# One scattered row per token instead of two, and every instruction placed anew, in a sparse attention layer on one core

## The chip, the cores and the metric

The kernel runs on one core of a Trainium2 chip. The metric is the time of one execution on the device in microseconds (us). The same program is executed several times; the median of the runs is given, and one execution is also recorded by the hardware profiler. Engines are named as in the profile: PE (TensorE), PEld (its weight loads), DVE (VectorE), ACT (ScalarE), POOL (GpSimd), SP (SyncE, which here only issues DMAs).

## The reference

There are 16 batches of 1024 tokens with 512 numbers each, and one 1024 x 1024 adjacency for all of them, in which every token has itself and a few neighbours.

```python
h = jnp.maximum(_layernorm(x, axis=-1), 0.0)
q = (h @ Wq + bq).reshape(b, n, 8, 64)      # k and v in the same way
scores = jnp.einsum('bihd,bjhd->bhij', q, k) / jnp.sqrt(64.0)
mask = jnp.where(adj == 0, -1e9, 0.0)
weights = softmax(scores + mask, axis=-1)
out = x + jnp.einsum('bhij,bjhd->bihd', weights, v)
```

Everything is in float32. Most of a row of the adjacency is zero, so that the softmax of a token runs over a handful of neighbours.

## The kernel before

**Sorting, once.** Tokens are sorted by their number of neighbours and cut into 8 tiles of 128. A tile t has `CAPS[t]` slots for neighbours, (11, 8, 6, 5, 4, 3, 3, 2), so that tiles of small degree do little. To sort, the kernel reads the adjacency, takes the degree of each token on DVE, and finds the rank of each token (`rank_of`, `ranks`), which is its row in sorted order. For each natural tile t of 128 tokens, `list_of(t)` (L1120, L1121) masks the rows of the adjacency with token numbers and takes the eight largest with one MAX8: the list of up to eight neighbours. Two facts about each token then have to go to its place in sorted order, through DRAM:

- the numbers: the token's own number and, for the first batch only, the two constants of its layernorm, scale and shift (`shift` computes the last). `tell(t)` scatters them, three floats for a token, into `told_table`;
- the list: whether the token is its own neighbour, and the eight neighbours. `spread(t)` scatters them, nine floats for a token, into `lists_table`.

Both are indirect DMAs that POOL issues (L1124), one for each tile and table, so sixteen. Once all eight of a table are done, `collect` (L1135) loads the table back in sorted order with one DMA of SP's queue. From the numbers, `perm_of` (L1142) makes `perm`, the list of token numbers in sorted order. With `perm`, POOL loads the tokens of all batches in sorted order (`load_x`, L1002), one indirect DMA for each tile, writes the results back (`put_out`, L1409), and fetches the adjacency rows of the longest tile again (`long_rows`, L1152), whose remaining neighbours are found by `long_blocks` and `longest`. From the lists, `spots` (L1147) and `slots` (L1240 and following) make `index`, the row numbers that the gathers use. While all this goes on, the first batch's k and v are computed in natural order (names that end in `_first`) and scattered by rank (L1095).

**Each batch.** For each of 8 tiles: layernorm (DVE sums, ACT L1037), four transposes by PE (`flip`, L1044), a copy of the transposed tile by ACT (`unflip`, L1049), and projections to k, v and q (`project`: a bias product L1055 and four float32 products L1057, which the profile counts as eight). The k and v of a tile go into one of three DRAM buffers of 1024 rows. Then the attention runs in 14 `UNITS` for a batch, a unit being up to four slots of one tile: `gather` (L1288) fetches the k|v rows of the neighbours, one indirect DMA for each slot, the own row by SP; DVE multiplies with q (L1298) and sums to scores (L1302); ACT takes exponents (L1306) and weighs v, eight activations for a slot (`weigh_s`, L1332), some slots by DVE (`weigh_v`, L1318); DVE, POOL and PE add the slots up (`fold` L1337, `add_up` L1356); DVE divides, and POOL or DVE adds x (`residual`, L1406). Tile 0 has a unit more, for tokens with more neighbours than slots (`pieces`, number -1). The projections of a batch run one batch ahead of its attention.

**The order of work.** It is written out by hand. Each operation has a place, a number in the table `PLACES`; `Plan.ordered()` sorts all operations by it and issues them in that order, and an engine executes its own in the order of issue. The kind `once` holds the sorting, `first` the natural-order k and v, `0`, `1` and `2` the first three batches, `3` every further one but two, `next` the last but one, `last` the final one; for batch b the number gets b times `PERIOD` = 95.290021 added. Waits between engines come from the dependencies.

Of the kernel before, what the change touches and what calls it, by code (L numbers as in the profile page):

```python
# [97 lines left out]
        list_of=(-13.2, -13.4, 13.93, 14.05, -4.33, -7.76, -9.88, 14.25,),  # L98
        tell=(-12.63, -16.97, -13.14, 9.24, 0.89, 16.11, 17.75, 19.88,),
        spread=(45.38, 47.45, 30.7, 45.48, 45.35, 30.46, 22.54, 45.26,),  # L100
        collect=(-9.17, 5.02,),
        others=(14.42,),
        perm_of=(0.42,),
        spots=(26.84,),
        long_rows=(30.4,),
        long_blocks=(16.58, 20.59, 22.61, 24.22, 24.98,),
        longest=(27.18, 29.37, 32.28, 35.43, 36.11, 39.52, 41.52, 44.79, 45.14,),
        count_pieces=(46.89,),
        first_piece=(122.72,),
        owners=(94.07,),  # L110
        flip_owners=(136.43,),
        copy_owners=(113.68,),
        list_pieces=(137.27,),
        pieces=(127.38,),
        slots=(142.24,),
        add_bias=(-19.2, -17.6,),
        spread_bias=(68.07,),
        copy_bias=(89.7,),
# [4 lines left out]
        norm=(75.49, 76.09, 77.09, 77.49, 79.89, 80.09, 80.34, 80.69,),  # L123
        flip=(75.49, 75.69, 76.49, 76.69, 78.69, 78.89, 90.39, 104.64,),
        unflip=(75.89, 76.49, 77.29, 77.89, 80.49, 80.72, 96.22, 97.88,),
        proj_kv=(75.89, 77.49, 76.29, 77.89, 76.89, 78.49, 79.09, 79.29, 86.87, 98.15, 99.79, 107.75, 135.06, 147.6, 153,
            148.32,),
        evict_kv=(76.89, 79.29, 77.69, 79.49, 78.09, 80.29, 80.4, 80.66, 96.1, 96.13, 96.42, 106.28, 154.55, 162.49, 169.71,
            172.46,),
        store_kv=(78.35, 116.17, 119.38, 125.35, 140.7, 146.55, 148.18, 147.06,),  # L130
        variance=(75.89, 76.89, 79.29, 81.69,),
        power=(75.69, 76.29, 78.29, 87.8,),
# [3 lines left out]
        load_x=(30.09, 30.5, 38.8, 45.21, 45.44, 47.92, 49.07, 49.69,),  # L136
        norm=(2.13, 2.31, 24.77, 49.09, 71.39, 77.14, 77.27, 78.66,),
        flip=(50.32, 51.95, 54.11, 55.9, 60.64, 67.45, 67.52, 68.48,),
        unflip=(27.69, 53.06, 72.64, 77.2, 79.54, 81.13, 82.77, 84.23,),
        queries=(67.49, 69.07, 115.56, 126.07, 127.49, 138.29, 148.67, 168.76, 169.97,),  # L140
        gather=(45.09, 65.92, 63.96, 81.66, 82.98, 67.8, 87.05, 86.63, 69.01, 87.14, 102.98, 103.26, 67.61, 108.86, 109.63,
            108.64, 107.92, 79.49, 116.69, 119.1, 130.36, 131.45, 130.44, 102.76, 142.21, 138.67, 142.4, 144.98, 150.63,
            142.37, 142.46, 108, 152.91, 152.09, 152.7, 153.37, 153.1, 152.82, 153.23, 171.08, 171.84, 155.19, 172.79,
            155.41, 171.17, 171.11,),
        multiply=(47.46, 64.59, 81.01, 107.03, 126.74, 113.33, 126.77, 141.63, 149.43, 155.18, 163.45, 170.22, 180.88,
            178.07,),
        score=(47.54, 67.41, 96.06, 111.76, 129.2, 117.87, 128.06, 146.83, 153.31, 155.84, 165.66, 174.39, 181.78, 195.93,),
        exponent=(92.19, 93.82, 105.44, 111.15, 115.51, 115.42, 115.56, 141.97, 143.4, 152.67, 166.31, 172.53, 173.27,
            183.23,),
        row_sums=(64.37, 70.18, 97.04, 118.27, 142.77, 160.52, 163.48, 203.64,),  # L150
        share=(64.49, 74.75, 101.56, 119.16,),
        weigh_v=(69.44, 130.54, 142.01, 144.6, 161.03, 163.57, 170.25, 175.36, 195.82,),
        weigh_s=(92.85, 101.83, 100.44, 95.75, 106.78, 112.94, 106.75, 115.48, 115.39, 115.45, 122.29, 116.89, 121.19, 119.7,
            142.94, 135.53, 142.97, 143.03, 144.58, 154.99, 152.31, 153.27, 163.13, 166.52, 165.91, 171.8, 172.93, 171.74,
            173.08, 173.04, 172.99, 174.92, 175.62, 181.86, 185.22, 185.42, 187.44,),
        fold=(71.91, 97.01, 97.07, 132.47, 137.68, 138.95, 141.69, 143.23, 145.64, 143.05, 153.79, 155.15, 156.82, 161,
            163.76, 171.2, 173.85, 175.66, 181.17, 186.5, 187.92, 183.84, 200, 202.21, 204.35, 204.53,),
        residual=(109.25, 124.53, 138.45, 141.77, 153.19, 171.14, 178.55, 219.35,),
        put_out=(129.95, 130.51, 141.35, 142.43, 153.4, 178.16, 179.5, 225.23,),
        join=(147.89, 161.06, 175.01,),  # L160
        scale=(148.16, 161.67, 176.53, 211.41,),
        copy_q=(145.23,),
        add_up=(188.54, 194.88, 203.87, 205.55,),
        more=(201.41,),
        pass_on=(203.77,),
        seen=(331.72,),
    ),
    1: dict(
        load_x=(-45.57, -43.85, -39.73, -39.1, -35.32, -8.38, 7.1, 14.11,),
        stats=(-63.36, -61.71, -54.75, -49.26, -50.34, -20.16, 1.69, 45.35,),  # L170
        norm=(-12.29, -8.07, -1.29, 11.92, 17.92, 21.28, 45.19, 45.66,),
        flip=(-14.6, 13.76, 33.62, 50.55, 65.56, 72.21, 73.87, 79.53,),
        unflip=(-6.21, -2.22, 15.4, 21.31, 28.65, 37.54, 57.61, 68.73,),
        proj_kv=(17.02, 20.04, 31.75, 42.81, 49.67, 52.6, 71.12, 55.79, 72.24, 74.1, 74.46, 79.5, 79.61, 83.24, 86.3, 90.4,),
        evict_kv=(-2.01, -35.87, 14.8, 20.07, 20.47, 37.41, 38.89, 36.39, 47.71, 60.13, 57.69, 63.79, 70.59, 76.3, 77.5,
            77.55,),
        store_kv=(7.84, 6.03, 7.72, 17.75, 21.65, 22.37, 41.88, 46.5,),
        variance=(-59.83, -48.24, 0.42, 46.54,),
        power=(-31.44, 7.33, 34.59, 50.93,),
        shift=(-56.77, -25.47, 22.23, 52.69,),  # L180
        queries=(92.98, 95.46, 99.76, 113.88, 114.01, 119.61, 134.23, 135.77, 151.42,),
        gather=(53.63, 85.6, 64.02, 85.49, 85.7, 72.03, 102.18, 95.44, 87.81, 104.49, 108.17, 108.68, 107.7, 109.8, 109.4,
            111.58, 112.73, 107.63, 119.79, 126.28, 135.9, 135.96, 135.93, 140.28, 147.73, 148, 149.33, 149.5, 150.8, 150.83,
            149.71, 142.94, 156.83, 157.14, 151.75, 157.7, 150.86, 150.89, 162.73, 165.24, 165.07, 165.98, 165.43, 166.72,
            176.54, 166.09,),
        multiply=(100.67, 106.6, 119.91, 124.46, 149.54, 145.64, 149.6, 154.01, 164.31, 168.95, 171.4, 175.59, 182.84,
            188.66,),
        score=(107.36, 108.32, 124.43, 142.56, 149.57, 145.7, 153.22, 157.27, 165.13, 170.5, 171.68, 182.66, 188.41, 193.53,),
        exponent=(101.25, 100.12, 106.42, 110.23, 116.2, 116.09, 136.58, 137.26, 142.79, 164.86, 172.22, 183.82, 187.9,
            189.8,),  # L190
        row_sums=(111.52, 118.48, 124.49, 145.67, 151.53, 163.54, 171.43, 223.45,),
        share=(112.04, 119.71, 124.55, 145.84,),
        weigh_v=(115.89, 145.87, 155.15, 158.81, 169.44, 171.46, 193.56, 188.61, 193.59,),
        weigh_s=(102.16, 107.3, 103.87, 104.01, 107.98, 108.93, 112.16, 116.05, 121.06, 115.46, 125.94, 135.88, 136.78,
            122.78, 137.3, 139.07, 140.95, 141.59, 137.36, 163.59, 164.34, 153.33, 167.75, 166.89, 171.97, 181.76, 182.84,
            176.37, 187.96, 186.35, 188.1, 189.16, 190.92, 190.49, 191.49, 191.11, 190.86,),
        fold=(119.37, 124.52, 136.3, 135.99, 136.05, 152.83, 147.47, 157.39, 160.24, 157.34, 165.19, 168.14, 169.06, 169.41,
            174.3, 178.51, 174.7, 177.42, 193.62, 193.65, 193.68, 198.47, 195.72, 204.29, 208.27, 212.87,),
        residual=(113.65, 130, 143.43, 153.45, 160.4, 179.56, 185.95, 209.42,),
        put_out=(129.97, 136.02, 156.67, 157.96, 166.22, 183.18, 187.67, 215.86,),  # L200
        join=(163.89, 169.49, 187.98,),
        scale=(164.12, 171.36, 188.49, 227.3,),
        copy_q=(144.08,),
        add_up=(188.22, 192.32, 197.88, 215.67,),
        more=(188.38,),
        pass_on=(191.08,),
        seen=(236.64,),
    ),
    2: dict(
        load_x=(-56.28, -51.47, -39.61, -36, -12.07, 6.83, 6.86, 40.79,),  # L210
# [34 lines left out]
        copy_q=(156.1,),  # L245
        add_up=(202.93, 206.57, 210.96, 218.78,),
        more=(187.77,),
        pass_on=(211.16,),
        seen=(311.13,),
    ),  # L250
    3: dict(
# [1356 lines left out]
```

## Time and profile before

| what | value |
|---|---|
| median of 3 runs | 1613.55 us (1610.17 to 1617.66) |
| profiled execution, own time | 1612.02 us |
| its span | 1609.9 us |
| mean granted PE clock | 0.992 |
| PE busy | 1572.1 us |
| DVE busy | 1518.2 us |
| ACT busy | 1444.8 us |
| POOL busy | 1258.7 us |

The span is the time between the first and the last instruction in the trace; the profiled execution's own time has some 2 us more around it. The busy time of an engine is a sum over the whole span. Register, branch and DMA-issuing instructions do not count as busy, except the indirect DMAs of POOL, which appear with the time that POOL spends on issuing them. The granted clock says how much of its full speed PE was allowed. Times within a timeline are counted from the start of the span.

### The profile page before, as it was taken

The page shows a single profiled execution, that of the slowest core. Times are in us where ns is not written, and L with a number is a line of the kernel's source. Part 1 is how long each engine was busy: PE and PEld are TensorE (multiplying, and loading weights), DVE is VectorE, ACT ScalarE, POOL GpSimd, SP SyncE. Part 2 cuts the span into 40 slices and gives each one's busy share as a digit, 9 for nine tenths or more (in the row PEclk, how much of TensorE's full clock was granted, in tenths as well). Part 3 has the DMA queues.
Part 4 walks back from the last instruction along what each step waited for, and adds up shares of the span by engine and source line. Part 5 has one row for each costly group of instructions (what it writes and reads, how often), then busy time and mean ns, then how long its engine had stood idle before and what let it go on. Part 6 is the DMA issues. An engine that isn't in the chain of part 4 may idle for free. (4 is left out here: it accounts for less than half of the span.)

```text
span 1609.9 us, 19515 instructions
## 1 busy us (share of the span) xinstructions
PE 1572.1 (98%) x4242; PEld 732.0 (45%) x4242; DVE 1518.2 (94%) x2075; ACT 1444.8 (90%) x5428; POOL 1258.7 (78%) x1185
## 2 busy tenths in 40 slices
PE   8999999999999999999999999999999999999687
PEld 4444444444444444444444444444444444444233
DVE  8889999999999999999999999999999999999897
ACT  4459999898999989899898989999998998989897
POOL 3777778887788888888788787878788887786666
PEclk9999999999999999999999999999999999999899
DMA  6499989999999999999999999999999999998886
GB/s 249 141 351 341 334 319 358 329 366 323 341 333 345 366 333 357 325 351 349 339 357 346 345 337 345 344 343 352 330 339 331 341 373 326 338 335 330 324 306 217
DMA packets 149876, 531.56 MB, mean 330 GB/s; under 512 B 19052, under 2 KB 19052, under 8 KB 149752
## 3 DMA queue, kind: packets, MB, share of 16 engines
q0 software_dynamic: 109840, 390.70, 67.9%
q1 hardware_dynamic: 39912, 139.56, 23.0%
q8 instruction: 35, 0.57, 0.1%
q14 instruction: 89, 0.73, 0.1%
HBM read 429.46 MB, written 100.72 MB: 329 GB/s over the span
## 5 line engine op out<-in xcount | busy, mean ns | idle before, releaser
L1332 ACT ACTIVATE g<-g,weights 128x64 f32<-128x64 f32 x4704 | 1160.3, 338 | 40.9 <-DVE weights L1311 37.8
L1288 POOL DMA_INDIRECT g<-kv,index x608 | 642.2, 1056 | 206.7 <-issue 163.2
L1057 PE MATMUL pq<-wq,hT 128*128 128x512 f32 x1024 | 462.4, 595 | 0.0
L1057 PE MATMUL pk<-wk,hT 128*128 128x512 f32 x960 | 431.7, 593 | 0.0
L1057 PE MATMUL pv<-wv,hT 128*128 128x512 f32 x960 | 431.4, 593 | 0.0
L1302 DVE TENSOR_REDUCE weights<-g 128x32 f32<-128x2048 f32 (+2 forms) x224 | 423.7, 1897 | 2.0
L1298 DVE TENSOR_TENSOR g<-g,pq 128x2048 f32<-128x2048 f32 (+2 forms) x208 | 388.7, 1870 | 28.1 <-DMA g<-kv 9.9
L1057 PEld LDWEIGHTS pq<-wq,hT 128*128 128x128 f32 x1024 | 195.8, 191 | 216.9 <-issue 213.2
L1057 PEld LDWEIGHTS pv<-wv,hT 128*128 128x128 f32 x960 | 182.4, 190 | 213.5 <-issue 210.6
L1057 PEld LDWEIGHTS pk<-wk,hT 128*128 128x128 f32 x960 | 182.7, 190 | 201.4 <-issue 196.8
L1337 DVE TENSOR_TENSOR g<-g 128x512 f32<-128x512 f32 (+1 forms) x301 | 253.9, 851 | 9.8 <-ACT g L1332 8.4
L1409 POOL DMA_INDIRECT out_dram<-x,perm x128 | 136.7, 1068 | 39.8 <-issue 30.6
L1002 POOL DMA_INDIRECT x<-in_x_dram,perm x128 | 135.8, 1061 | 34.9 <-issue 32.5
L1337 POOL TENSOR_TENSOR g<-g 128x512 f32<-128x512 f32 x90 | 115.0, 1284 | 17.6 <-DVE g L1337 10.5
L1037 ACT ACTIVATE h<-x,shift,rstd 128x512 f32<-128x512 f32 x120 | 96.5, 807 | 12.0 <-DVE shift L1027 11.4
L1318 DVE TENSOR_TENSOR g<-g,weights 128x512 f32<-128x512 f32 x143 | 101.9, 716 | 1.1 <-ACT weights L1306 0.6
L1356 PE MATMUL acc<-g,ident 128*128 128x512 f32 x170 | 84.4, 612 | 14.6 <-ACT g L1332 10.8
L1044 PEld LDWEIGHTS pht<-ident,h 128*128 128x128 f32 x512 | 63.2, 141 | 68.6 <-issue 52.7
L1406 POOL TENSOR_TENSOR x<-x,o 128x512 f32<-128x512 f32 x64 | 81.9, 1280 | 9.4 <-DVE o L1392 5.0
L1049 ACT COPY hT<-pht 128x512 f32<-128x512 f32 x128 | 73.0, 571 | 16.3 <-PE pht L1044 16.2
L1011 DVE BATCH_NORM_STATS2 st<-x 128x6 f32<-128x512 f32 x120 | 81.2, 677 | 1.6 <-DMA x<-in_x_dram,perm 1.6
L1044 PE MATMUL pht<-ident,h 128*128 128x128 f32 x512 | 76.5, 273 | 3.2 <-ACT hT L1049 1.9
(242 smaller groups left out, 1080.2 us busy)
## 6 DMA issues: line engine op xcount, KB each, us to landing
g<-kv SPq DMA_DIRECT2D x128, 512.0 KB, 7.7
kv<-kvt SPq DMA_DIRECT2D x120, 512.0 KB, 6.9
g<-kv,index POOLq DMA_INDIRECT x608, 6.9
adj<-in_adj_dram SPq DMA_DIRECT2D x8, 512.0 KB, 8.2
x_first<-in_x_dram SPq DMA_DIRECT2D x8, 256.0 KB, 6.0
x<-in_x_dram,perm POOLq DMA_INDIRECT x128, 5.5
out_dram<-x,perm POOLq DMA_INDIRECT x128, 6.6
wk<-in_L_gnn_Wk_dram SPq DMA_DIRECT2D x1, 1024.0 KB
```

Source lines behind the costliest of these rows:

```text
L1002: nc.gpsimd.indirect_dma_start(out=X[n][:], out_offset=None, in_=x_rows, in_offset=on(ap=perm[:, t : t + 1], axis=0), element_offset=b * N * D
L1037: nc.scalar.activation(HN[n], X[n], AF.Relu, bias=shift, scale=scale)
L1044: nc.tensor.transpose(PH[n][:, c, :], hn[:, ts(c, P)], ident)
L1057: nc.tensor.matmul(pt, HT[n][:, c, :], W[name][:, c, :], start=(apart and c == 0), stop=(n != -NT and c == DC - 1))
L1288: nc.gpsimd.indirect_dma_start(out=G[i][:, s].rearrange("p j d -> p (j d)"), out_offset=None, in_=KV[b % len(KV)][:], in_offset=on(ap=inde ...
L1298: nc.vector.tensor_tensor(k, k, Q[b, t][:, None, :].to_broadcast([P, count, D]), ALU.mult)
L1302: nc.vector.tensor_reduce(weights[:, w, :], heads(G[i][:, :count, 0, :]), AX.X, ALU.add)
L1318: nc.vector.tensor_tensor(v, v, own.to_broadcast([P, n, H, HD]), ALU.mult)
L1332: nc.scalar.activation(v[:, h, :], v[:, h, :], AF.Identity, scale=weights[:, c + s, h : h + 1])
L1337: engine.tensor_tensor(v[:, 0:n], v[:, 0:n], v[:, first : first + n], ALU.add)
L1356: nc.tensor.matmul(ACC[b, home], owner_t if t < 0 else ident, v[:, s, :], start=(u == added_up(b, B, home)[0] and s == 0), stop=(u == adde ...
L1409: nc.gpsimd.indirect_dma_start(out=out_rows[t], out_offset=on(ap=perm[:, t : t + 1], axis=0), in_=X.pop(b * NT + TILES.index(t))[:], in_of ...
```

## The change

The two tables become one of twelve floats for a token: own number, scale, shift, whether it is its own neighbour, eight neighbours. `spread` is gone; `tell(t)` scatters the twelve floats at once, eight indirect DMAs instead of sixteen, and so depends on `list_of(t)` and on `shift`. One `collect` loads the table back, and both `perm_of` and `spots` depend on it. The list columns stand behind the numbers, in columns 3 to 11. Besides, every number in `PLACES` is replaced, of all kinds from `once` to `last`. `PERIOD`, the buffers, the units and the division of work among engines stay as they are, and a steady batch issues the same instructions as before.

```diff
     for t in range(NT):
         add(("list_of", t), "DVE", [("ends",), ("no_diagonal", t)], [sources])
-        add(("tell", t), "POOL", [("ranks",), ("shift", (t - NT) // 2)])
-        add(("spread", t), "POOL", [("list_of", t)])
-    add(("collect", "told"), "SP", [("tell", t) for t in range(NT)])
-    add(("collect", "lists"), "SP", [("spread", t) for t in range(NT)])
+        add(("tell", t), "POOL", [("list_of", t), ("shift", (t - NT) // 2)])
+    add(("collect",), "SP", [("tell", t) for t in range(NT)])
...
-    add(("perm_of",), "DVE", [("collect", "told")])
-    add(("spots",), "DVE", [("collect", "lists"), ("setup", 2)])
+    add(("perm_of",), "DVE", [("collect",)])
+    add(("spots",), "DVE", [("collect",), ("setup", 2)])
...
-        itself, near = 0, slice(1, 9)
-        width_of = dict(told=3, lists=9)
...
+        itself, near = 3, slice(4, 12)
+        before, after = (const.tile([P, NT, 12], F32, tag=name, name=name) for name in ("before", "after"))
+        table = nc.dram_tensor("told_table", [N, 12], F32).ap()
+        views = dram_disjoint_views(table, NT)
...
-                nc.gpsimd.memset(before["lists"], 0.0)
-                nc.gpsimd.tensor_copy(before["told"][:, :, own], place)
+                nc.gpsimd.memset(before, 0.0)
+                nc.gpsimd.tensor_copy(before[:, :, own], place)
...
+        def tell(t):
             nc.gpsimd.indirect_dma_start(
-                out=views[name][t], out_offset=on(ap=spot_i[:, t : t + 1], axis=0), in_=before[name][:, t, :], in_offset=None
+                out=views[t], out_offset=on(ap=spot_i[:, t : t + 1], axis=0), in_=before[:, t, :], in_offset=None
             )
...
-        def collect(name):
-            nc.sync.dma_start(after[name], tables[name].rearrange("(p t) c -> p t c", t=NT))
+        def collect():
+            nc.sync.dma_start(after, table.rearrange("(p t) c -> p t c", t=NT))
```

And of the places, the sorting's one of the steady batches' (kind `3`) and two of the last batch's:

```diff
-        list_of=(-13.2, -13.4, 13.93, 14.05, -4.33, -7.76, -9.88, 14.25,),
-        tell=(-12.63, -16.97, -13.14, 9.24, 0.89, 16.11, 17.75, 19.88,),
-        spread=(45.38, 47.45, 30.7, 45.48, 45.35, 30.46, 22.54, 45.26,),
-        collect=(-9.17, 5.02,),
-        others=(14.42,),
-        perm_of=(0.42,),
-        spots=(26.84,),
-        long_rows=(30.4,),
+        list_of=(-13.2, -13.4, -13.64, -5.49, 29.82, -11.73, -13.5, 9.88,),
+        tell=(-2.47, -2.81, -2.2, 0.46, 20.99, -0.47, 0.43, 15.84,),
+        collect=(-3.23,),
+        others=(32.93,),
+        perm_of=(31.19,),
+        spots=(32.96,),
+        long_rows=(26.22,),
...
-        flip=(-10.81, -8.95, 19.94, 35.21, 52.47, 61.74, 70.98, 73.85,),
+        flip=(-7.65, -5.54, 33.09, 40.88, 46.68, 59.19, 70.43, 81.4,),
...
-        queries=(262.15, 252.79, 252.44, 222.65, 210.97, 194.72, 156.92, 125.39, 127.47,),
+        queries=(296.72, 265.33, 253.44, 241.69, 218.97, 184.96, 182.93, 120.67, 143.27,),
...
-        copy_q=(115.48,),
+        copy_q=(139.29,),
```

Of the last three pairs, `flip` is of the kind `3`, one number for each tile from 7 to 0; `queries` and `copy_q` are of the kind `last`.

## The prediction

> **What bounds the kernel now.** I read the page's busy times first, then the same by stage, then the timeline of each engine at the two ends. In the page, the busy line and the slices:
>
> ```profile
> PE 1572.1 (98%) x4242; PEld 732.0 (45%) x4242; DVE 1518.2 (94%) x2075; ACT 1444.8 (90%) x5428; POOL 1258.7 (78%) x1185
> ...
> PE   8999999999999999999999999999999999999687
> ```
>
> TensorE is the full engine, and only the first slice and the last three fall below nine tenths. By stage (columns: window, length, busy PE, PEld, DVE, ACT, POOL, granted clock, DMA share, GB/s; instruction counts in brackets):
>
> ```profile
> 0.00:113.00 113.00, 104.90 (x311) 51.48 (x312) 94.55 (x263) 51.41 (x105) 70.10 (x90) 0.98 0.68 245
> 685.00:780.00 95.00, 95.00 (x258) 44.41 (x257) 90.59 (x119) 89.37 (x340) 78.13 (x73) 1.00 0.95 351
> 1447.00:1543.00 96.00, 77.82 (x191) 34.01 (x190) 87.19 (x85) 85.50 (x332) 62.59 (x60) 0.91 0.87 323
> 1543.00:1610.00 67.00, 56.88 (x139) 24.94 (x137) 54.35 (x73) 54.20 (x230) 44.42 (x43) 0.97 0.73 257
> ```
>
> In the middle PE has no gap: one batch costs the PE work of one batch, about 95.3 us (24 projections of 8 x 0.429 + 0.215 = 3.65, 8 flips of 0.44, the rest adds and small products). Time can be won or lost in three ways: PE starts its steady run later or earlier; it comes to wait inside that run; or the last 107 us, where PE idles 96 - 77.8 + 67 - 56.9 = 28 us and DVE and ACT are at 81 to 91%, get shorter or longer.
>
> **What the Trainium skill says.** "DMA: Bandwidth & Descriptors", section on the SWDGE path, fits a DMA's time as about 2.0 us plus bytes/436e3. A scatter of 128 rows of 12 B lands after 2.4 us at the median in this trace, one of 36 B after 2.4 too, so a 48 B row should cost no more. "TensorE: Matmul & The Clock Gate", section on the clock gate, has PE at half rate after an idle window of about 3.4 us and at full rate after about as long busy. The trace agrees in kind: after a gap of 9.2 us two adds took 2.05 us, 0.86 elsewhere. But a gap of 1.91 us too was followed by a projection of 5.19 us instead of 3.60.
>
> **Part 1: eight scatters fewer.** On POOL (start, us, instruction, idle before):
>
> ```profile
> 45.91 0.96 POOL L1124 DMA_INDIRECT told_table<-before_told,spot_i  x1 [0.30 <-issue]
> ...
> 70.86 0.96 POOL L1124 DMA_INDIRECT lists_table<-before_lists,spot_i  x1 [0.30 <-issue]
> ...
> 87.15 1.01 POOL L1288 DMA_INDIRECT g<-kv,index  x1 [0.19 <-issue]
> ```
>
> Each takes 0.96 + 0.30 = 1.26 us of POOL; eight are 10.1 us. All lie before the first gather, in a stretch where POOL issues back to back. On SP two collects become one (a load of 2.7 us either way; 384 B for each partition instead of 96 and 288). The zeroing of 128 x 96 values instead of 128 x 72 is early work on POOL ahead of the ranks, under the wait for the adjacency: nothing.
>
> **Part 2: the permutation waits for the lists.** Before, `perm_of` needed the numbers only. DVE shows both collects:
>
> ```profile
> 50.73 0.17 DVE L1142 CAST perm<-after_told 128x8 int32<-128x8 f32 x1 [2.30 <-DMA after_told<-told_table]
> ...
> 76.12 0.75 DVE L1147 COPY spot<-after_lists 128x8 f32<-128x8 f32 x7 [1.73 <-DMA after_lists<-lists_table]
> ```
>
> Now one row carries both, and the last tile's list must be found first. The lists cost 1.21 + 1.23 = 2.4 us of DVE each; the first ends near 38.8, and in the new order of DVE all eight run with little between them, so the last (tile 4) ends near 55.7. Its scatter is issued at 55.8, lands 2.1 later, the collect takes 2.7: `perm` at about 60.6, **10 us later** than 50.73. DVE waits about 4.9 us for it (before: 2.30 and 1.73). Behind it on DVE stand only `others`, spots and slots, then the layernorm sums of loads that need `perm` themselves; behind the collect on SP stand the own rows of the first gathers, not due before 80. Behind `perm` on POOL stand the store of three k|v tiles that were not waiting for it, then `long_rows` and the eight loads of batch 0. Nine issues of 1.27 us give 62.2 to 72.3 for them (before: the first eight loads at 53.2 to 74.7, with scatters between). So the first loads are later and the last ones earlier. Spots and slots now follow `perm` at once (62 to 66 instead of 76 to 80).
>
> PE in this stretch: the sixteen projections of batch 0's k and v in natural order run to about 76 in both orders. Then before had
>
> ```profile
> 79.08 0.66 PE L1044 MATMUL pht<-ident,h 128*128 128x128 f32 x4 [1.91 <-ACT hT L1049]
> ...
> 79.89 5.19 PE L1057 MATMUL pq<-wq,hT 128*128 128x512 f32 x8
> ...
> 102.53 0.39 PE L1055 MATMUL pq<-bias_parts,chosen 128*128 128x512 bf16 x1 [0.70 <-DVE g L1298]
> ```
>
> that is 1.91 + 1.6 (clock) + 0.70 = 4.2 us lost. In the new order I follow the flips of batch 0: a load lands 5.5 us after its issue, the norm takes 0.81 and the flip waits on it, and I find gaps of about 2.5, 1.4 and 0.6 us, 4.5 us, plus up to 2 of lost clock. **The start of the steady run moves by 0 to +3 us; I take +2.** A loss of 10 us (the whole delay of `perm`) is excluded as long as PE has the natural-order projections to do until 76.
>
> **Part 3: the first gather.** POOL has ten fewer microseconds of issues but two natural k|v stores wait for ACT's evictions; I get the first gather at 82.5 instead of 87.15 and the first multiply at 91.4 instead of 96.45. PE does not wait for the attention there; only the 0.70 us behind the multiply can come from it. By the fourth multiply (113.5 in both) the lead is gone, since the new order of DVE puts more layernorm work between. Worth nothing by itself.
>
> **Part 4: places of the steady batches.** Each batch issues the same instructions; only their order on each engine changes. What decides is whether PE meets an operand that is not ready. Counting PE work between the end of a flip and the projection that reads it, the shortest distance of a steady batch is 4.94 us now (tile 1) and in the new order 4.09 (tile 7, now 7.74), beside 4.94 again. In between ACT must copy the flipped tile (0.57 us, L1049) and, being in order, finish what it has begun; one neighbour slot is eight activations, 2.02 us in this trace. With one slot ahead 4.09 - 0.57 - 2.02 leaves 1.5 us; with two it is 0.5 short. One early batch of the kernel before has a distance of 4.09 too, and PE waits nowhere there. The other distances are 7.3 us and more, and projections of queries reach PE at nearly the same points as before (that of the pieces 3.7 us later). I take **0**, from 0 to +25 (a stall of up to 2 us in 13 batches); a gain is excluded, since PE has no gap to lose there.
>
> **Part 5: the tail.** The last k|v projection ends at 1503.7. Now
>
> ```profile
> 1512.91 2.05 PE L1356 MATMUL acc<-g,ident 128*128 128x512 f32 x2 [9.20 <-ACT g L1332]
> ...
> 1515.76 4.06 PE L1057 MATMUL pq<-wq,hT 128*128 128x512 f32 x8
> ```
>
> so the last batch's first query sits on PE behind an add that waits 9.2 us for ACT, and the multiply behind it waits once more for ACT's copy of that query:
>
> ```profile
> 1524.93 2.29 DVE L1298 TENSOR_TENSOR g<-g,pq 128x2048 f32<-128x2048 f32 x1 [4.98 <-ACT q L1279]
> ```
>
> In the new order the query stands directly behind the last projection, and the multiply waits for its gathers alone, which land near 1521 if they are issued as now (first at 1508.75). That is 4 us earlier on DVE. After 1543 DVE and ACT share the limit, so some is given back: **-3 us**, bounded by -6 (DVE's whole 4.98 and a warm PE clock) and +4 (DVE and ACT left with a worse interleaving of 14 units).
>
> **Sum.** 1612.0 (profiled execution: span 1609.9 and 2.1 around it) + 2 + 0 - 3 = 1611. The median shown is 1613.55, 1.5 above that execution, so the middle of my case is 1611 to 1612.5; I say 1612.
>
> **Rivals.** *Slower:* ACT stands two or three slots behind at the flip of tile 7 (or an equal distance elsewhere that a schedule with 90% busy ACT and 95% busy DVE cannot hold). From the point at which the wait passes 0.6 us a batch, 13 batches make more than 8 us; at 1 us it is 1612 + 13 = 1625, at 1.5 us 1632. For it: DVE and ACT leave only 5 us of slack in a batch and every position is new. Against it: in the trace of before PE waits nowhere between 110 and 1503 at the same kind of distances. *Faster:* the earlier gather is kept to the first batch's end (5 us), and the tail gives the full 4: 1613.5 - 9 = 1604. Against it: PE's clock, not DVE's, sets the steady run, so a lead at the start has no way to the end. *Late permutation:* the loads that come 10 us later leave PE without flips at 76: +5 and a cold clock, 1618, still inside the band of no change.
>
> **Numbers.** What a measurement of this kernel can tell from no change is about 0.5%, 8 us. No change (cases of the sum and of the late permutation): 0.46, own range 1606 to 1620. Slower, by stalls of PE or a longer tail: 0.36. Faster: 0.18. The range goes from 1603 to 1630.
>
> **What would show it.** Right: `perm` near 60 us; sixteen scatters become eight; first gather near 82; PE without gaps from about 115 to 1504; the first multiply of the last batch near 1521. Wrong: PE waits on ACT's flipped tile or on an eviction in the windows of the middle, a window of 95 us that holds less than 95 us of PE, or a tail longer than 107 us after the last k|v projection.

## The result and the profile after

The changed kernel takes 1620.17 us (median of 8 runs, 1618.75 to 1623.73), the kernel before, run beside it, 1616.29 us (8 runs). The ratio is 1.0036, with a 95% interval of 1.0020 to 1.0053: **slower by 0.36%**, about 6 us. A second set of the changed kernel gave 1621.37 us and again 1.0036 [1.0024, 1.0048]. The forecast was 1612 us, a hair faster than before; the measured time lies inside its range, on the other side. The profiled execution took 1619.76 us, with a span of 1618.1, near its median; that of before (1612.02) lies 1 to 4 us under the medians of its kernel. So the two traces differ by 8.2 us of span where the medians differ by 4 to 6. In one later set (e16 and e17 below) the kernel before took 1631.1 us, 15 to 18 us more than in all others, for a reason that no trace here shows, and e17, the changed kernel with one operation moved, was 0.4% faster than it: the 0.36% holds for the other sets.

The busy line of the page, and stages of the changed kernel (columns as in the prediction: window, length, then busy PE, PEld, DVE, ACT, POOL, granted clock, DMA share, GB/s):

```profile
PE 1573.4 (97%) x4209; PEld 731.5 (45%) x4242; DVE 1516.5 (94%) x2075; ACT 1447.7 (89%) x5428; POOL 1247.9 (77%) x1177
```

```profile
0.00:113.00 113.00, 103.05 (x304) 50.41 (x309) 91.28 (x255) 52.44 (x106) 62.18 (x81) 1.00 0.66 242
208.00:303.00 95.00, 93.90 (x251) 43.53 (x254) 89.55 (x111) 87.53 (x331) 73.80 (x70) 1.00 0.92 338
303.00:398.00 95.00, 91.80 (x248) 42.40 (x248) 90.23 (x112) 87.22 (x329) 74.31 (x69) 1.00 0.89 325
683.00:778.00 95.00, 94.89 (x256) 44.34 (x257) 91.40 (x119) 89.47 (x342) 76.90 (x72) 1.00 0.94 342
```

The middle is as full as before. POOL has eight instructions less and 11 us less work. What is new is the stretch from 208 to 398 us: PE is idle for 95 - 93.90 + 95 - 91.80 = 4.3 us there. The same windows of the kernel before:

```profile
208.00:303.00 95.00, 94.80 (x257) 44.07 (x256) 90.29 (x119) 89.80 (x346) 77.58 (x71) 1.00 0.94 340
303.00:398.00 95.00, 94.88 (x258) 44.10 (x257) 92.68 (x117) 86.91 (x330) 76.18 (x72) 1.00 0.94 341
```

0.3 us. In the second trace of the changed kernel (c_after below) it is 3.7 us. The timeline of PE shows the two longest of these waits, in batches 2 and 3:

```profile
319.56 0.39 PE L1048 MATMUL pq<-bias_parts,chosen 128*128 128x512 bf16 x1 [1.67 <-DVE g L1285]
343.02 3.70 PE L1050 MATMUL pv<-wv,hT 128*128 128x512 f32 x8 [1.17 <-ACT kvt L1068]
```

A query waits for a DVE multiply that still reads the PSUM bank of an earlier query, and a projection to v waits for ACT's copy out of the k|v bank that it is to take. Neither waits for a flipped tile.

To see where the time sits, one PE instruction of each batch serves as a mark, the query of the pieces (tile -1). Before and then after, for batches 0 and 3:

```profile
155.67 1.02 PE L1275 MATMUL pq_-1_1404<-q,owner 128*128 128x512 f32 x2
...
440.63 1.02 PE L1275 MATMUL pq_-1_3801<-q,owner 128*128 128x512 f32 x2
```

```profile
160.14 1.02 PE L1262 MATMUL pq_-1_1423<-q,owner 128*128 128x512 f32 x2
...
449.62 1.02 PE L1262 MATMUL pq_-1_3843<-q,owner 128*128 128x512 f32 x2
```

The new order has one projection more ahead of the mark (3.65 us), so of the 4.47 us by which it is later at batch 0 0.82 were lost at the start. In the same way the loss is 1.65 us at batch 1, 4.8 at batch 2 (two projections more there), 5.34 at batch 3 and 5.77 at batch 8; the last k|v projection ends at 1508.77 us instead of 1503.71. After it the changed kernel needs 109.3 us to the end of the span, the kernel before 106.2. **The account of the pair of traces: start +0.82, batches 1 to 3 (from the mark of batch 0 to that of batch 3) +4.52, the rest of the run about -0.3, the end +3.1, together 8.2.** It is one pair of executions; which of these sums come again in other traces is said below.

At the end, on PE and DVE of the changed kernel:

```profile
1508.82 3.60 PE L1050 MATMUL pq<-wq,hT 128*128 128x512 f32 x8
```

```profile
1524.15 2.28 DVE L1285 TENSOR_TENSOR g<-g,pq 128x2048 f32<-128x2048 f32 x1
...
1543.51 2.29 DVE L1285 TENSOR_TENSOR g<-g,pq 128x2048 f32<-128x2048 f32 x1 [3.22 <-issue]
...
1551.62 2.27 DVE L1285 TENSOR_TENSOR g<-g,pq 128x2048 f32<-128x2048 f32 x1
```

The query is where the prediction saw it, directly behind the last projection. The first multiply starts 15.4 us after that projection's end (before: 21.2), the fourth, which waits 3.22 us, after 34.7 (35.6), the fifth after 42.8 (41.9). The fifth of the kernel before:

```profile
1545.58 2.28 DVE L1298 TENSOR_TENSOR g<-g,pq 128x2048 f32<-128x2048 f32 x1
```

The lead of 5.8 us is gone within four units, and the rest is behind.

### The profile page after: what moved, and what is told of

The parts are those of the page before. It is cut to its first block, busy times and chain, and to the rows that moved or that the text cites. A ratio compares the mean times of both kernels' runs of the same rounds, so it can differ in the third digit from the quotient of the medians.

```text
span 1618.1 us, 19496 instructions
## 1 busy us (share of the span) xinstructions
PE 1573.4 (97%) x4209; PEld 731.5 (45%) x4242; DVE 1516.5 (94%) x2075; ACT 1447.7 (89%) x5428; POOL 1247.9 (77%) x1177
## 5 line engine op out<-in xcount | busy, mean ns | idle before, releaser
L1319 ACT ACTIVATE g<-g,weights 128x64 f32<-128x64 f32 x4704 | 1164.9, 347 | 34.7 <-DVE weights L1298 31.3
L1275 POOL DMA_INDIRECT g<-kv,index x608 | 634.3, 1043 | 215.9 <-issue 162.0
L1285 DVE TENSOR_TENSOR g<-g,pq 128x1536 f32<-128x1536 f32 (+2 forms) x208 | 389.1, 1871 | 20.8 <-DMA g<-kv 5.8
L1396 POOL DMA_INDIRECT out_dram<-x,perm x128 | 141.5, 1106 | 39.9 <-issue 30.0
```

Of the source, the lines that this page charges most:

```text
L1275: nc.gpsimd.indirect_dma_start(out=G[i][:, s].rearrange("p j d -> p (j d)"), out_offset=None, in_=KV[b % len(KV)][:], in_offset=on(ap=inde ...
L1285: nc.vector.tensor_tensor(k, k, Q[b, t][:, None, :].to_broadcast([P, count, D]), ALU.mult)
L1319: nc.scalar.activation(v[:, h, :], v[:, h, :], AF.Identity, scale=weights[:, c + s, h : h + 1])
L1396: nc.gpsimd.indirect_dma_start(out=out_rows[t], out_offset=on(ap=perm[:, t : t + 1], axis=0), in_=X.pop(b * NT + TILES.index(t))[:], in_of ...
```

## The experiments

Two theories stood at first. The places theory: one table costs nothing, and the new numbers in `PLACES` lose the time, in batches 1 to 3 and at the end. The table theory: the permutation, 11 us later, makes the first batches late, and PE pays for that. (Not quite every number in `PLACES` is new: some 120 of about 1950 are the same in both kernels, nearly all of them of the sorting and of the first loads ahead of the lists.)

"Before" is the median of the kernel before on the same chip at the same time.

| kernel | us | before | ratio, 95% interval |
|---|---|---|---|
| e1_table_only | 1625.95 | 1614.95 | 1.0074 [1.0060, 1.0088] |
| e2_places_only | 1654.20 | 1614.95 | 1.0242 [1.0220, 1.0263] |
| e3_after_old_end | 1687.83 | 1614.95 | 1.0470 [1.0452, 1.0488] |
| e4_after_old_ramp | 1724.06 | 1614.95 | 1.0677 [1.0662, 1.0691] |
| e5_after_ramp_moves | 1620.43 | 1613.82 | 1.0039 [1.0027, 1.0051] |
| e6_before_last_query | 1614.08 | 1613.82 | 0.9992 [0.9984, 1.0001] |
| e7_after_unit_order | 1619.76 | 1613.82 | 1.0035 [1.0022, 1.0047] |
| e8_table_stores_first | 1624.04 | 1613.82 | 1.0052 [1.0036, 1.0068] |
| e9_table_hidden | 1622.35 | 1615.22 | 1.0043 [1.0027, 1.0058] |
| e10_before_first_multiply | **1609.21** | 1615.22 | **0.9965 [0.9953, 0.9977]** |
| c_after | 1621.37 | 1615.22 | 1.0036 [1.0024, 1.0048] |
| e11_after_evictions_early | 1620.06 | 1613.17 | 1.0041 [1.0026, 1.0057] |
| e12_after_outputs_early | 1619.65 | 1613.17 | 1.0044 [1.0029, 1.0060] |
| e13_after_both | 1621.25 | 1613.17 | 1.0047 [1.0035, 1.0060] |
| e14_less_act | 1621.52 | 1614.13 | 1.0045 [1.0024, 1.0066] |
| e15_less_dve | 1615.76 | 1614.13 | 1.0013 [1.0001, 1.0024] |
| e16_dve_time_back | 1623.52 | 1631.10 | 0.9952 [0.9937, 0.9968] |
| e17_others_early | 1623.88 | 1631.10 | 0.9960 [0.9942, 0.9978] |

e16 and e17 are read by their traces alone.

**The table without the new places (e1, e8, e9).** e1 has the table of the changed kernel and the places of before, with what the dependency demands:

```diff
-        tell=(-12.63, -16.97, -13.14, 9.24, 0.89, 16.11, 17.75, 19.88,),
-        spread=(45.38, 47.45, 30.7, 45.48, 45.35, 30.46, 22.54, 45.26,),
-        collect=(-9.17, 5.02,),
+        tell=(-12.63, -13.0, 14.0, 14.1, 0.89, 16.11, 17.75, 19.88),
+        collect=(5.02,),
...
-        perm_of=(0.42,),
+        perm_of=(14.3,),
```

> One table of twelve floats, one scatter for each tile, all places as before, except that perm_of stands behind the last list and the scatters behind their lists. Places theory (the new numbers in PLACES cost the time, the table costs nothing): within 2 us of before; perm at 58 to 62 us instead of 50.7, yet PE without waits from 115 us on, and the last k|v projection ends at 1502 to 1506 us. Table theory (perm eleven us later makes the layernorms of the first batches late, and PE waits for what depends on them): 4 to 8 us slower than before, with PE waits of 3 us or more between 208 and 398 us.

It lost 11 to 12 us, so the places theory failed here. But the time was not lost where the table theory had it: from 208 to 398 us PE was idle for 0.1 us. Nearly all of it lies ahead of 115 us, at one wait on PE's timeline:

```profile
65.18 0.58 PE L1048 MATMUL pk_first<-bias_parts,chosen 128*128 128x512 bf16 x1 [12.41 <-ACT kvt_first L1068]
```

ACT's copy of a natural-order k waited for a buffer, whose scatter stood on POOL behind scatters of the table, which waited for the last list. e8 moves three such stores ahead:

```diff
+MOVED = {('store_kv', -7): 0.5, ('store_kv', -6): 0.6, ('store_kv', -5): 0.7}
-            result.append(PLACES[kind][spot[0]][at] + PERIOD * (b or 0))
+            result.append(MOVED[key] if key in MOVED else PLACES[kind][spot[0]][at] + PERIOD * (b or 0))
```

> As e1_table_only, with the scatters of three natural k|v tiles ahead of the table's scatters on POOL, in time in which POOL waited for a list. If e1 lost its time because those stores, standing behind scatters that wait for the last list, kept ACT's eviction and so PE waiting (12.4 us): that wait falls below 2 us and the whole is 8 to 12 us faster than e1, about as before or a little slower. If it lost it to the late permutation itself: PE then waits for the flips of batch 0 instead, and it is less than 4 us faster than e1.

The 12.4 us wait is gone, the time is not: against before, e8 is 1 to 4 us better than e1, and PE now waits for the flips of batch 0, 5.05 and 2.85 us, whose tokens are loaded by the permutation at 63.8 us. This is the second answer of its expectation. e9 besides puts the natural-order work of PE and ACT ahead of these flips, as the changed kernel does:

```diff
+    ('proj_kv', -2, 1): 17.0, ('proj_kv', -1, 1): 27.5, ('flip', 0): 41.4, ('proj_kv', -1, 0): 42.1, ('flip', 1): 42.3,
+    ('evict_kv', -2, 0): 2.0, ('evict_kv', -2, 1): 2.05, ('norm', 0): 4.1, ('norm', 1): 14.6, ('unflip', 0): 15.5,
...
```

> As e8_table_stores_first, and besides, PE and ACT do what they have left of the natural k and v ahead of the first flips and norms of batch 0, as in the changed kernel: seven operations of PE and fifteen of ACT change places, all before 95 us; every later place is that of before. Places theory (the table is free where other work covers the wait for the permutation, and the changed kernel loses its 6 us later, in batches 1 to 3 and at the end): within 3 us of before, at 1612 to 1617 us, PE idle below 1.5 us between 113 and 398 us, 106 us after the last k|v projection. Table theory: still 5 us or more slower than before.

Still 0.43% slower, and all of it ahead of 113 us (0.3 us idle from 208 to 398 us, 105.4 us after the last k|v projection). PE's largest wait is further back now, at another flip of batch 0:

```profile
97.32 2.30 PE L1060 MATMUL pht<-ident,h 128*128 128x128 f32 x8 [6.08 <-ACT h L1053]
```

So one table costs 7 to 12 us in an order made for two, in the three ways tried. The changed kernel's own order of the start pays 0.82 for it. A new order of the start is thus part of the price of the table; that every later place had to change too is not shown.

**The places without the table, and places of two kernels joined (e2, e3, e4).** e2 takes the places of all batches from the changed kernel and the rest from before, e3 and e4 put kinds of before into the changed kernel. As orders of different kinds don't fit, `ordered()` was changed in them so that, where no engine's next operation can be issued, the ready operation with the least place leaves its queue early.

```diff
+            if not ready:
+                for engine, queue in waiting.items():
+                    for i in queue[head[engine] :]:
...
+                _, i, new = min(ready)
```

> Two tables and sixteen scatters, and the sorting's own places, as before; the places of every batch, the first to the last, as in the changed kernel. Places theory: 4 to 8 us slower than before, PE waits of 3 us or more between 208 and 398 us on evictions and on a multiply, the last k|v projection ends at 1507 to 1510 us, the rest after it takes 109 us. Table theory: within 2 us of before.

> The changed kernel with the places of the last two batches as before. Places theory, in which 3 of the us are lost after the last k|v projection: 3 us faster than the changed kernel (1617 us at 1620 for that), the last k|v projection still at 1507 to 1510 us, the rest after it 106 us instead of 109.3. Rival (the end is set by what all engines still have to do, whatever the order, and the 3 us are the spread of single executions): as the changed kernel, the rest 109 us.

> The changed kernel with the places of the first three batches (kinds 0, 1, 2) as before. Places theory: PE's waits between 208 and 398 us (4.3 us in the changed kernel) fall below 1 us, the last k|v projection ends at 1503 to 1506 us instead of 1508.8, and the whole is 3 to 5 us faster than the changed kernel. Table theory: the waits stay, no faster.

All three missed every expectation by far, at the seams: e2's PE is idle for 13.4 us between 113 and 208 us, e3's for 20.3 between 1348 and 1443, e4's for 20.0 between 113 and 208 and for 25.5 between 303 and 398. Their times say nothing on the theories; they say that the places of one kind hold only beside the neighbours that they were made for.

**The waits of batches 1 to 3 (e5, e11).** In the changed kernel, six of 33 k|v projections between 205 and 400 us find their bank freed only 0.05 to 0.33 us before they take it; in the kernel before none does, and the least margin is 0.87 us. (Margin: from the end of the eviction, which is the copy out of the bank, to the first float32 product of the next projection into that bank, the second one further on; counted from the two traces.) e5 moves three evictions and one query (its list is shown), e11 sixteen evictions on ACT by one to seven steps, one on DVE, and the same query:

```diff
+MOVED = {('queries', 2, 1): 342.0, ('evict_kv', 27, 0): 339.15, ('evict_kv', 17, 1): 221.65, ('evict_kv', 22, 1): 273.0}
```

> The changed kernel with four operations moved by one to four steps in their own engine's order, so that none of the four largest waits of PE between 208 and 398 us (0.47, 0.42, 1.67 and 1.17 us) has its cause left: three evictions ahead of the weighting or the multiply they stood behind, one query behind one k|v projection. Places theory: those waits go, the last k|v projection ends 3.0 to 3.7 us earlier, at about 1505.3 us, and the whole is about 3 us faster than the changed kernel. Rival (DVE and ACT are late there altogether, the waits only come up a few steps later): other waits of PE take their place, and the whole stays within 1 us of the changed kernel.

> The changed kernel with sixteen evictions of batches 1 to 3 moved ahead of the weighting that they stood behind on ACT (by one to seven steps), one on DVE, and one query behind one k|v projection on PE. Bank theory (PE takes one of two k|v banks back 0.1 to 0.4 us after its eviction in six places, and a late eviction stops it): PE's waits between 113 and 398 us fall from 3.8 to 4.4 us to below 1.5, the last k|v projection ends 2.5 to 3.5 us earlier, and the whole is 2.5 to 3.5 us faster than the changed kernel. Rival (DVE and ACT are late altogether): other waits take their place, no faster.

Both came out as their rivals say. PE's idle time between 208 and 398 us stayed at 4.2 and 4.5 us, with other waits; in e11 two of them are for k|v banks that ACT has not left:

```profile
342.21 3.70 PE L1072 MATMUL pv<-wv,hT 128*128 128x512 f32 x8 [1.72 <-ACT kvt L1090]
...
346.99 0.38 PE L1070 MATMUL pk<-bias_parts,chosen 128*128 128x512 bf16 x1 [1.07 <-ACT kvt L1090]
```

**Which engine is late there (e14, e15).** Each takes work from one engine in batches 0 to 2 and leaves every order as it is.

```diff
-            for h in range(H):                                            # e14, weigh_s
+            for h in range(0 if b < 3 and s == 0 and count == 4 else H):
+            if b < 3:                                                     # e15, weigh_v
+                return
+            if n == 2 and i < 3 * NU:                                     # e15, fold
+                return
```

> The changed kernel; in batches 0 to 2 the first slot of each unit of four slots is left unweighed: ACT has 6 slots of 2.0 us less to do in each of these batches, DVE all of its own. If ACT is the late engine in the early batches: PE's waits between 113 and 398 us fall from 3.8 to 4.4 us to below 1.5 and the last k|v projection ends about 3 us earlier. If DVE is: the waits stay above 3 us.

> The changed kernel; in batches 0 to 2 DVE leaves out its own weighting of v and the first fold of each unit of four slots, some 13 us of DVE in each of these batches; ACT does all of its own. If DVE is the late engine: PE's waits between 113 and 398 us fall below 1.5 us. If ACT is: they stay above 3 us. If both e14 and e15 take them away, each engine waits for the other, and the order couples them.

The two windows of e14, then of e15:

```profile
208.00:303.00 95.00, 94.04 (x255) 43.74 (x254) 91.67 (x111) 76.38 (x285) 74.38 (x70) 1.00 0.93 337
303.00:398.00 95.00, 91.57 (x247) 42.36 (x246) 89.90 (x111) 75.91 (x283) 74.36 (x69) 1.00 0.89 326
```

```profile
208.00:303.00 95.00, 94.86 (x257) 44.15 (x256) 78.60 (x100) 88.50 (x339) 72.00 (x70) 1.00 0.94 344
303.00:398.00 95.00, 93.77 (x254) 43.52 (x253) 82.10 (x104) 87.74 (x335) 74.08 (x72) 1.00 0.92 338
```

ACT with 11 us less to do in each window changes nothing: 4.4 us of PE idle. DVE with 8 to 11 less brings it to 1.4, the last k|v projection to 1505.4 us, and the whole to 1.0013 of before. **Of these two DVE is the late engine**, also where PE's wait names an eviction by ACT. ACT gets its weights from DVE's scores. POOL was not tested in this way.

**Whose fault DVE's lateness is (e16, e17).** DVE's wait for the permutation is the first thing that the table lengthens (below). e16 gives DVE 7 us back just behind it by leaving out four multiplies, e17 moves 1.28 us of work into the wait.

```diff
+            if i < 4:                      # e16, multiply
+                return
```

```diff
+MOVED = {('others',): 30.5}              # e17
```

> The changed kernel without the multiplies of the first four units of batch 0 (1.2, 1.75, 1.75 and 2.3 us of DVE between 92 and 117 us); everything else and every order stays. Debt theory (the wait for the permutation leaves DVE some 4 us behind, and PE pays for it in batches 1 to 3): PE's waits between 113 and 398 us fall from 3.8 to 4.4 us to below 1.5 us, and the whole is about 3 us faster than the changed kernel. Rival (DVE's order in batches 1 to 3 makes PE wait wherever DVE starts from): the waits stay above 3 us.

> The changed kernel with others, 1.28 us of DVE that need no permutation, issued ahead of perm_of, in DVE's wait for it. Debt theory: DVE is 1.3 us less behind, PE's waits between 113 and 398 us fall by about 1 us, the whole by at most 1 us, less than these rounds can tell. Rival: the same waits.

The longest wait in e16:

```profile
323.71 0.39 PE L1048 MATMUL pq<-bias_parts,chosen 128*128 128x512 bf16 x1 [2.89 <-DVE g L1287]
```

PE is idle for 5.6 us between 208 and 398 us in e16 and 4.7 in e17, in the same places as in the changed kernel. The debt theory expected less, but neither run put DVE ahead. In e16 DVE's fifth score starts at 123.8 us and its tenth at 159.1, in the changed kernel at 123.1 and 156.0: other waits took the 7 us. In e17 the first flip of batch 0 waits 5.61 us instead of 1.93, and the mark of batch 0 comes at 165.6 us instead of 160.1.

Other traces settle more. e1, e8 and e9 have the late permutation and the old places of the batches, and PE is idle for 0 to 0.3 us between 208 and 398 us. So the waits come with the new places and not with the late permutation. And in the first pair of traces DVE falls behind late, within batches 1 and 2. Its 24th and 29th scores, before and after:

```profile
250.17 2.27 DVE L1302 TENSOR_REDUCE weights<-g 128x32 f32<-128x2048 f32 x1
...
284.56 1.22 DVE L1302 TENSOR_REDUCE weights<-g 128x16 f32<-128x1024 f32 x1
```

```profile
251.71 2.28 DVE L1289 TENSOR_REDUCE weights<-g 128x32 f32<-128x2048 f32 x1
...
291.21 1.21 DVE L1289 TENSOR_REDUCE weights<-g 128x16 f32<-128x1024 f32 x1
```

DVE is 1.5 us later than before at the first of these and 6.7 at the second, ahead of PE's longest wait at 319.56 us. Which of its operations stand at the wrong place stays open.

**The end (e6, e10, e7, e12, e13).** e6 and e10 do in the kernel before what the prediction's part 5 is about. e6 moves the query only; e10 also lets the first multiply be issued ahead of ACT's copy of that query, so that it no longer waits for it. The order on each engine is the same in e6 and e10; only which of the two readers of the query is issued first differs.

```diff
+MOVED = {('queries', 15, 0): 1533.35, ('copy_q', 15): 1547.65, ...}     # e6
+MOVED = {('queries', 15, 0): 1533.35, ('copy_q', 15): 1554.5, ...}      # e10
```

> The kernel before with one move on PE: the first query of the last batch directly behind the last k|v projection, ahead of the add that waits 9.2 us; the first multiply does not wait for ACT's copy of it. The prediction's part 5: the first multiply of the last batch starts 4 us earlier, near 1521 us, and the whole is 2.5 to 4 us faster than before. Rival (the gathers of the last batch, one after the other from 1508.7 us, set the pace until about 1540): the multiply is earlier, but from the third or fourth unit on nothing is, and the whole is within 1 us of before.

> As e6_before_last_query, in which the first multiply of the last batch still waited for ACT's copy of the query; here it is issued ahead of that copy and waits for its gathers alone. The prediction's part 5: the multiply starts near 1520 us instead of 1525, and the whole is 2.5 to 4 us faster than before. Rival (the gathers, or what DVE and ACT have left, set the pace further on): the multiply starts near 1520 us, the whole stays within 1.5 us of before, and the multiplies from the fifth on start as before, counted from the last k|v projection.

In e6 the multiply still waited 4.97 us for ACT's copy, at 1525.47 us, and nothing moved: PE's query 12 us earlier is worth nothing by itself. In e10:

```profile
1518.65 2.28 DVE L1309 TENSOR_TENSOR g<-g,pq 128x2048 f32<-128x2048 f32 x1
...
1542.15 2.28 DVE L1309 TENSOR_TENSOR g<-g,pq 128x2048 f32<-128x2048 f32 x1
```

16.2 us after the last k|v projection, about as in the changed kernel, and here the lead is kept: its fifth multiply starts after 39.7 us (before 41.9, changed 42.8), the last after 86.4 (89.0, 90.0). e10 is 5.6 us faster than before by the ratio, more than expected, and the fastest kernel of the study. The traces show less of it: the end is 103.9 us in e10, 106.2 in before, 107.9 in e6, so 2.3 to 4.0 us; the rest is not shown.

e7 undoes the one difference in DVE's order of units in the last batch (12 and 13), e12 takes seven late operations of batch 14 from the end of POOL's queue:

```diff
+MOVED = {('multiply', 222): 1560.4, ('multiply', 223): 1566.4, ('gather', 222, 1): 1544.05, ...}      # e7
+MOVED = {('residual', 14, 0): 1632.35, ('put_out', 14, 7): 1632.45, ('put_out', 14, 5): 1632.55, ...}  # e12
```

> The changed kernel with units 12 and 13 of the last batch in the order of before: the last two gathers of unit 12 ahead of those of 13 on POOL, its multiply and score first on DVE. If the longer end (109.3 us after the last k|v projection instead of 106.2) comes from DVE's wait of 3.2 us for the gathers of unit 12: 2 to 3 us faster than the changed kernel. If it comes from the order of all that follows: within 1 us of it.

> The changed kernel with the last residual and six output scatters of batch 14 moved on POOL from the end of the last batch into a time in which POOL waited 7.5 us for a buffer. If the end is longer by POOL's queue of scatters (POOL ends 2.8 to 4.3 us after DVE's last residual, 2.1 before the change): POOL ends within 2.2 us of DVE and the whole is 1 to 2 us faster than the changed kernel. If DVE and ACT themselves end later: within 1 us of it, and the lead of the first multiply is still gone by the fifth.

> Both edits together: the sum of the two if each is real, 3.5 to 5.5 us faster than the changed kernel, which is within 2 us of the kernel before.

Neither gains. In e7 the fifth multiply starts 45.1 us after the last k|v projection. In e12 POOL does end 1.9 us behind DVE's last residual (4.3 in the changed kernel, 2.1 before), and its trace ends 107.9 us after the last k|v projection instead of 109.3; but DVE's last residual ends 100.3 us after that projection as in the changed kernel (100.2, before 98.8), and the kernel is no faster. e13, both e11 and e12, gains nothing either. So the lead of the first multiply is lost on DVE between the first and the fifth unit, and POOL's last scatters add to it in the first trace; which of the many differences of order loses the lead stays open.

c_after asks whether both losses belong to the kernel:

> The changed kernel as it is, for a second trace beside the first. If the PE waits of 4.3 us between 208 and 398 us and the 109.3 us after the last k|v projection belong to its places, they come again within 1 us; if they are the spread of single executions, they do not.

3.7 us of PE idle between 208 and 398 us and 110.4 us after the last k|v projection. The first comes again everywhere: 3.7 to 5.9 us in eleven traces with the new places of these batches (the two of the changed kernel, e3, e5, e7, e11 to e14, e16, e17), 0 to 1.0 in six with the old ones (before, e1, e6, e8, e9, e10). (e2, behind its seam, has 6.4, e15 with less DVE work 1.4.) The second is less firm. The new places of the last batch take 107.0 to 110.9 us in eleven traces (the two of the changed kernel, e2, e5, e7, e11 to e16) and 104.3 in e17; the old ones 105.4 to 106.5 in four (before, e1, e8, e9), 107.3 in e3. By the medians of these groups the end costs about 1.5 us, not the 3.1 of the first pair. What does come again is that the lead is lost: the fifth multiply starts 41.5 to 45.1 us after the last k|v projection in the eleven, after 41.9 in before and 39.7 in e10.

## Why the prediction was wrong

**What bounds the kernel** was right: PE's run, its start and the end.

**Part 1** was right and, as it said, worth nothing alone. Eight scatters are gone, those of 48 B land after 2.2 us (12 and 36 B: 2.4), as the Trainium skill ("DMA: Bandwidth & Descriptors", the SWDGE path) led one to expect, and the first gather starts at 83.40 us (said 82.5):

```profile
57.18 0.96 POOL L1117 DMA_INDIRECT told_table<-before,spot_i  x1 [0.30 <-issue]
...
83.40 0.94 POOL L1275 DMA_INDIRECT g<-kv,index  x1 [0.98 <-PE pq L1050]
```

**Part 2** was right within its bounds. On DVE:

```profile
62.08 0.17 DVE L1129 CAST perm<-after 128x8 int32<-128x8 f32 x1 [6.18 <-DMA after<-told_table]
```

11.4 us later than before (said 10), a wait of 6.2 (said 4.9). PE's gaps:

```profile
78.12 1.36 PE L1037 MATMUL pht<-ident,h 128*128 128x128 f32 x8 [1.93 <-ACT h L1030]
...
85.17 1.36 PE L1037 MATMUL pht<-ident,h 128*128 128x128 f32 x8 [1.39 <-ACT h L1030]
...
91.79 3.70 PE L1050 MATMUL pk<-wk,hT 128*128 128x512 f32 x8 [0.73 <-ACT hT L1042]
```

1.93, 1.39 and 0.73 us where 2.5, 1.4 and 0.6 were worked out, and no clock was lost behind them in this trace (in others it was, see the last section). I took +2 and the marks give +0.82. e1, e8 and e9 show how much hangs on that order: 7 to 12 us. The rival of the late permutation was thus real, but the new order avoids it; that its 1618 us came nearest to the 1620 measured is luck. (A slip of reading: two adds in a row take 1.02 us elsewhere in the trace of before, not 0.86; after the gap of 9.2 us they still took twice as long.)

**Part 3** was right: the first multiply at 92.83 us (said 91.4), the fourth at 113.78 (before 113.52), the lead gone.

**Part 4 is the step that failed.** It said 0, and 4.52 us were lost between the marks of batches 0 and 3. In the steady batches 0 is nearly what the marks give, 0.4 us over five of them (batch 3 to 8). But I counted distances in steady batches only, and only from a flip to the projection that reads it. The loss is where batches 0 to 2, whose places are kinds of their own, are at work, up to the projections of batch 3, and PE waits there for banks: one that a multiply still reads, and k|v banks that an eviction has not left. The distance to count was also that from one use of a bank to the next, on DVE as well as on PE, batch by batch. The slower rival had the sign and the wrong place, number of batches and engine: it put a wait of 1 us or so in each of 13 batches, at the flips of tile 7, on ACT. e14 shows that ACT doesn't matter and e15 that DVE does. Three of the signs of being wrong that the prediction lists did come: a wait on an eviction, windows with less than 95 us of PE, an end of more than 107 us.

**Part 5 had the right event and the wrong worth.** The first multiply came earlier by 5.8 us where I said 4. Alone, in e10, that is worth 5.6 us by the ratio, not the 3 I took. In the changed kernel it is worth nothing, since the lead is gone by the fifth multiply: I named "a worse interleaving of 14 units" as the bound of +4 and then took the middle of the gain. The term measured +3.1 in the first pair instead of -3, and about +1.5 over all traces.

**The sum.** +2, 0 and -3 were said; +0.8, +4.2 (batches 1 to 3 and the rest) and +3.1 were found in the first pair.

## What to carry to other kernels

When an order is replaced as a whole, walk it for every buffer that an operand's readiness does not show: count, for each pool with two banks, the work between one use and the next, also on the engines that free the bank, and do it for the first batches and the last one apart from the steady ones. An early start of one operation in a chain in order is a gain only if what follows is in the order to use it; test it alone. And joining two transfers makes both as late as the later one: what waited for the earlier must have other work, here a whole new order of the start.

## What the hardware showed that was not expected

PE's loss of clock behind a short gap goes with the single execution, not with the kernel. In the trace of before a gap of 1.91 us was followed by a projection of 5.19 us instead of 3.60. e10 has the same order there and the same gap, and loses nothing:

```profile
79.57 0.66 PE L1055 MATMUL pht<-ident,h 128*128 128x128 f32 x4 [1.91 <-ACT hT L1060]
...
80.28 3.60 PE L1068 MATMUL pq<-wq,hT 128*128 128x512 f32 x8
```

In the first trace of the changed kernel the gaps of 1.93 and 1.39 us were followed by projections of 3.60, and the granted clock was 1.00 over the first 113 us instead of 0.98. e11 has the same order there, and loses 1.15 us:

```profile
77.29 1.51 PE L1059 MATMUL pht<-ident,h 128*128 128x128 f32 x8 [1.92 <-ACT h L1052]
...
79.45 4.75 PE L1072 MATMUL pq<-wq,hT 128*128 128x512 f32 x8
```

Further on, a wait of 2.06 us in c_after was followed by a projection of 5.29 us, the one of 2.89 in e16 by 3.60. So the gap's length alone does not decide it, and all of these gaps are shorter than the idle window of about 3.4 us in the Trainium skill ("TensorE: Matmul & The Clock Gate", the clock gate). What decides it no run here shows. The 1.6 us of clock that the prediction counted at the start of the kernel before come and go in the same way.

A wait's named releaser was not the late engine: PE's waits in batches 1 to 3 name ACT and DVE by turns, and 11 us less of ACT work in each of two windows left 4.4 us of them, as many as before.

Two engines read the last batch's first query. With the same order on each engine, DVE's multiply waited 4.97 us for ACT's copy where the copy was issued first (e6), and not at all where the multiply was (e10); by the ratios that is worth some 4.4 us.
